# Wide attention spread over the narrow heads of the batch two before it, with norms batch by batch and their roots by Newton's method

## The chip, the cores and the metric

The kernel runs on one core of one Trainium2 chip. The metric is the device time in microseconds (us) from a launch; several runs are summed up by their median. The core has TensorE (PE in the profile, with its weight loads as PEld), VectorE (DVE), ScalarE (ACT), GpSimd (POOL) and SyncE (SP). Each engine works through its own queue in order; a semaphore makes one wait for another.

## The reference, cut to what matters

The input x has 8 batches of 512 tokens of width 128. All arithmetic is float32.

```
x = x + layernorm(attention(layernorm(x)))     # one wide head of 128, causal, rotary q and k
x = x + layernorm(ffn(layernorm(x)))
ffn(h): n = rmsnorm(h) * g1
        c = n @ w_down                         # 128 -> 64
        x' = h + attention of 16 narrow heads of width 4 over c, @ w_up
        t = rmsnorm(x') * g2
        probs = softmax(t @ router_w); top 2 of 8 experts, gates normalised
        return x' + sum over experts of gate * (silu(t @ w1) * (t @ w3)) @ w2
layernorm(x) = (x - mean) / sqrt(var + 1e-5);  rmsnorm(x) = x / sqrt(mean(x*x) + 1e-5)
```

## The kernel before, in words

Tokens lie on the 128 partitions, so a batch is NT = 4 tiles of 128x128. `x_all` and `h_all` hold all 32 tiles in on-chip memory. PSUM is dealt out as three buffers of two banks (tag `wide`), one single bank (tag `bank`), and one bank for the narrow heads' output (`po1`). All transposes and small products share the single bank; all score tiles share the three wide buffers.

**Stage 1, wide attention.** `ln_stats` takes mean and variance of 16 tiles at once (two groups of four batches), with a square root on ScalarE and a reciprocal on VectorE (`root`, L174). For each batch `attn_front` (L222) normalises, transposes, makes q and k (`pq`, each with a half-swapped copy, multiplied by the rotary table into `two` and added on POOL into `roped`) and v. `attn_back` (L248) makes causal scores two query tiles at a time, their negated maximum on VectorE, the exponential on ScalarE, transposes the probabilities (`pT`), multiplies by v (`po`) and by the output weights (`pr`). `between(gr)` (L302) then norms four batches, adds them to x and takes the norms of the next block. The loop at L732 issues the front of batch b+1 ahead of the back of batch b. This stage is ordered by the framework's own planner.

**Stage 2, narrow heads.** The order of this stage is written out by hand under `manual_schedule` (L837). A unit is one group of four heads of one batch: 8 batches x 4 groups = 32 units. `period(n)` (L758) interleaves three units: for v = n+1 the row-wise scores, which give each query's maximum (`rowwise`, `highest`: masks on TensorE, reduction on VectorE); for u = n the column-wise scores and exponentials (`columnwise`, `weights`: exponential on ScalarE) and their product with the values (`weigh`); for w = n+2 the copies into padded tiles on POOL (`values`, `queries`, `keys`) and the transposes through the single bank (`turn_q`, evacuated by VectorE; `turn_k` and `turn_m`, by ScalarE). `lower` splits the maxima into bf16 thirds on POOL, and `turn_m` of the next period reads them. A period uses the wide buffers eleven times, in the order 3A, 3C, 2A, (0,0), 2C, (0,1), 1AC, (1,0)+(3,0), 0AC, (1,1)+(3,1), 2; the letters are pairs of heads, the digits tiles of queries (row-wise) or of keys (column-wise).

Between these pieces stand calls of `aside()` (L747), four in a period. Each takes one step from a list of generators: `side` first, then `later`. On `side` come `ffn_front(b)` (L329: rms scaling `hs`, its transpose `hT`, the product `pc`, q, k and v `pqkv`, rotary, bf16 thirds on POOL) and `ffn_back(b)` (L552: `foT`, `pn`, `onT`, `pu`). On `later` comes `route(0)` (L588: rms statistics of 16 tiles with ScalarE's squares, router, top two).

**Stage 3, experts.** The planner orders `experts(b)` (L671), 64 experts-by-batch in all, with `route(1)` and, for each batch, `finish` (L719: layernorm, add on POOL, store).

Of the kernel before, what the change touches and what calls it, by code (L numbers as in the profile page):

```python
# [9 lines left out]
BF16 = mybir.dt.bfloat16  # L10
AF = mybir.ActivationFunctionType
# [3 lines left out]
P = 128  # L15
# [7 lines left out]
def kernel(  # L23
# [150 lines left out]
    def root(dst, src):  # L174

        sd = stat.tile([P, src.shape[1]], F32, tag="sd", name="sd")
        nc.scalar.activation(sd, src, AF.Sqrt)
        nc.vector.reciprocal(dst, sd)

    def ln_stats(src, n0, tag, n=GT):  # L180
# [5 lines left out]
        for i in range(n):  # L186
            nc.vector.bn_aggr(mv[:, i, :], st[:, i, :])
        ve = stat.tile([P, n], F32, tag="ve", name=f"ve_{tag}_{n0}")
        nc.vector.tensor_scalar(ve, mv[:, :, 1], EPS, None, ALU.add)
        rstd = stat.tile([P, n], F32, tag=f"rstd_{tag}", name=f"rstd_{tag}_{n0}")  # L190
        root(rstd, ve)
        return mv, rstd
# [7 lines left out]
    def rms_stats(src, n0, tag):  # L200

        ss = stat.tile([P, GT], F32, tag="ss", name=f"ss_{tag}_{n0}")
        for i in range(GT):
            sq = work.tile([P, D], F32, tag="sq", name=f"sq_{tag}_{n0}_{i}", bufs=1)
            nc.scalar.activation(
                sq, src[:, n0 + i, :], AF.Square, accum_out=ss[:, i : i + 1]
            )
        ve = stat.tile([P, GT], F32, tag="ve", name=f"vr_{tag}_{n0}")
        nc.vector.tensor_scalar(ve, ss, 1.0 / D, EPS, ALU.mult, ALU.add)
        rs = stat.tile([P, GT], F32, tag=f"rms_{tag}", name=f"rms_{tag}_{n0}")  # L210
        root(rs, ve)
        return rs
# [9 lines left out]
    def attn_front(b, st):  # L222
        xn = work.tile([P, NT, D], F32, tag="xn", name=f"xn_{b}")
        for t in range(NT):
            ln_apply(xn[:, t, :], x_all[:, b * NT + t, :], st, (b % GB) * NT + t)
        ps = transposed(xn, f"xnT_ps_{b}")
        xnT = work.tile([P, T], F32, tag="xnT", name=f"xnT_{b}")
        nc.scalar.copy(xnT, ps)
        roped = []
        for i in range(2):  # L230
# [3 lines left out]
            two = deep.tile([P, 2, T], F32, tag="pk", name=f"two_{b}_{i}", bufs=5)  # L234
            nc.vector.tensor_tensor(two, pq, ropea, ALU.mult)  # L235
            r = work.tile([P, T], F32, tag=f"roped{i}", name=f"roped_{b}_{i}")
            nc.gpsimd.tensor_tensor(r, two[:, 0, :], two[:, 1, :], ALU.add)  # L237
            roped.append(r)
        pv = bank(f"pv_{b}")
# [4 lines left out]
        v = work.tile([P, NT, D], F32, tag="v", name=f"v_{b}")  # L244
        nc.scalar.copy(v, pv.rearrange("p (t d) -> p t d", d=D))
        return roped[0], roped[1], v

    def attn_back(b, q, k, v):  # L248
        probs = []
        sums = work.tile([P, NT], F32, tag="sums", name=f"sums_{b}")  # L250
        for half in range(NT // 2):
# [8 lines left out]
            for i in range(2):  # L260
# [8 lines left out]
                probs.append(p)  # L269
        pT = work.tile([P, NT, T], F32, tag="pT", name=f"pT_{b}", bufs=1)  # L270
        for t in range(NT):
# [8 lines left out]
            )  # L280
        po = bank(f"po_{b}")
# [7 lines left out]
        nc.vector.reciprocal(rinv, sums)  # L289
        pr = bank(f"pr_{b}")  # L290
        for t in range(NT):
# [4 lines left out]
            h_all[:, b * NT : (b + 1) * NT, :],  # L296
# [3 lines left out]
        )  # L300

    def between(gr):  # L302

        n0 = gr * GT
        st = ln_stats(h_all, n0, "r")
        for i in range(GT):
            ln_apply(h_all[:, n0 + i, :], h_all[:, n0 + i, :], st, i)
        for b in range(GB):
            n = slice(n0 + b * NT, n0 + (b + 1) * NT)
            nc.gpsimd.tensor_tensor(x_all[:, n, :], x_all[:, n, :], h_all[:, n, :], ALU.add)  # L310
        st = ln_stats(x_all, n0, "h")
        for i in range(GT):
            ln_apply(h_all[:, n0 + i, :], x_all[:, n0 + i, :], st, i)
        return rms_stats(h_all, n0, "h")
# [14 lines left out]
    def ffn_front(b, rs):  # L329
        hs = work.tile([P, NT, D], F32, tag="xn", name=f"hs_{b}")  # L330
        for t in range(NT):
            i = (b % GB) * NT + t
            nc.vector.tensor_scalar(
                hs[:, t, :], h_all[:, b * NT + t, :], rs[:, i : i + 1], None, ALU.mult
            )
        yield
# [251 lines left out]
    def route(gr):  # L588
        n0 = gr * GT
        rs = rms_stats(h_all, n0, "t")  # L590
# [137 lines left out]
    sts = [ln_stats(x_all, 0, "x")]  # L728
    roots = []
    front = attn_front(0, sts[0])  # L730
# [27 lines left out]
    def period(n):  # L758
# [49 lines left out]
        if w:  # L808
            w.turn_q()
# [117 lines left out]
```

## Time and profile before

| what | us |
|---|---|
| median of 3 runs | 1009.24 (1004.33 to 1009.9) |
| the profiled execution | 1003.33 |
| its span, first to last instruction | 1001.5 |
| mean granted TensorE clock | 0.939 of full |
| first row-wise score of stage 2 starts | 219.05 |
| first expert product starts | 647.99 |
| TensorE / VectorE / ScalarE / POOL busy | 858.0 / 564.5 / 426.8 / 190.9 |

The page gives busy time of each engine and, in 40 slices of 25 us, busy tenths of each engine and the clock that TensorE was granted in tenths. A window row gives, for one stretch, its length, then for each engine the busy time with the number of instructions, then the granted clock, the DMA share and GB/s. A timeline row gives start, time, engine, line, operation, output <- inputs with shapes, and in brackets how long the engine was idle before it and what ended that.

### The profile page before, as it was taken

How to read it: one execution, taken by the hardware profiler on the slowest of the kernel's cores; microseconds unless marked ns; L12 is line 12 of the kernel's file. 1: busy time of each engine (PE TensorE's matmuls, PEld its weight loads, DVE VectorE, ACT ScalarE, POOL GpSimd, SP SyncE). 2: the span in 40 equal slices, each digit the busy share in tenths (PEclk: the TensorE clock that was granted, in tenths of full speed). 3: DMA queues.
4: the chain of work that ended last, by engine and by line, in shares of the span. 5: the costliest groups of instructions: out<-in, count | busy, mean ns of one | idle time of the engine just before them, and what ended most of it. 6: DMA issues, size and time to landing. Idle time of an engine off the chain costs nothing.

```text
span 1001.5 us, 14809 instructions
## 1 busy us (share of the span) xinstructions
PE 858.0 (86%) x5888; PEld 493.5 (49%) x5888; DVE 564.5 (56%) x1287; ACT 426.8 (43%) x668; POOL 190.9 (19%) x476
## 2 busy tenths in 40 slices
PE   2777568739989898986989988899999999999996
PEld 1444345414444444444444544366666666666664
DVE  6444773385666556564656675255654545545454
ACT  0212361234665566667665656542432323323231
POOL 5211211054242414141424221000000000000000
PEclk9999987657999999998999998899999999999999
DMA  9000000000000000000000000000000000000000
GB/s 252 1 0 1 0 1 0 1 1 1 1 2 2 1 1 2 2 2 1 1 1 2 1 1 1 1 2 0 11 11 1 11 1 11 11 1 11 1 11 10
DMA packets 14293, 9.34 MB, mean 9 GB/s; under 512 B 1200, under 2 KB 14064, under 8 KB 14224
## 3 DMA queue, kind: packets, MB, share of 16 engines
q1 hardware_dynamic: 12640, 7.34, 2.6%
q10 hardware_dynamic: 1296, 0.92, 0.3%
q8 instruction: 46, 0.75, 0.3%
q14 instruction: 23, 0.19, 0.1%
q0 software_dynamic: 288, 0.14, 0.1%
HBM read 6.30 MB, written 2.10 MB: 8 GB/s over the span
## 4 chain that ended last, share of the span: by engine, by line
PE 72%; ACT 10%; DVE 9%; issue 6%; DMA 2%; POOL 1%; SPq 0%; ACTq 0%; POOLq 0%; DVEq 0%
PE ph L677 20%; PE py L693 10%; PE po L544 8%; ACT pk L537 6%; PE sT L509 5%; PE sT L530 4%; PE sm L461 3%; PE po L283 3%; PE pq L233 3%; DVE nm L481 2%; PE sm L474 2%; DVE h_all L196 2%; PE mT_ps L432 2%; PE kT_ps L432 1%; PE pT_ps L274 1%
## 5 line engine op out<-in xcount | busy, mean ns | idle before, releaser
L481 DVE TENSOR_REDUCE nm<-sm 128x2 f32<-128x1024 f32 (+2 forms) x192 | 200.4, 1045 | 129.5 <-PE sm L474 125.5
L537 ACT ACTIVATE pk<-sT 128x1024 f32<-128x1024 f32 x160 | 163.6, 1027 | 89.9 <-PE sT L530 86.5
L685 ACT ACTIVATE sil<-ph 128x512 f32<-128x512 f32 x128 | 75.8, 597 | 228.1 <-PE ph L677 207.5
L686 DVE TENSOR_TENSOR hid<-sil,ph 128x512 f32<-128x512 f32 x128 | 87.5, 687 | 116.2 <-ACT sil L685 116.0
L693 PEld LDWEIGHTS py<-w2s,hid 128*128 128x128 f32 x1024 | 124.3, 192 | 31.6 <-issue 26.1
L677 PE MATMUL ph<-tT_all,w3s 128*128 128x512 f32 x256 | 131.3, 595 | 0.0
L677 PE MATMUL ph<-tT_all,w1s 128*128 128x512 f32 x256 | 131.1, 594 | 0.0
L693 PE MATMUL py<-w2s,hid 128*128 128x128 f32 x1024 | 124.8, 275 | 1.2 <-DVE h_all L702 1.2
L509 PE MATMUL sT<-mT,kT 39*128 39x384 bf16 (+3 forms) x512 | 67.1, 311 | 43.8 <-ACT pk L537 34.8
L544 PE MATMUL po<-pk,vpad 128*32 128x512 f32 (+3 forms) x1024 | 91.6, 454 | 0.0
L702 DVE SCALAR_TENSOR_TENSOR h_all<-py,gate_all,h_all 128x128 f32<-128x128 f32 x256 | 72.5, 344 | 28.4 <-PE py L693 28.2
L677 PEld LDWEIGHTS ph<-tT_all,w3s 128*128 128x128 f32 x256 | 48.2, 190 | 58.3 <-issue 58.2
L724 POOL TENSOR_TENSOR y<-y,x_all 128x512 f32<-128x512 f32 x8 | 10.2, 1271 | 349.0 <-DVE y L196 310.0
L461 PE MATMUL sm<-kT,qT 36*128 36x256 bf16 (+3 forms) x512 | 74.4, 312 | 2.3 <-ACT kT L439 1.4
L474 PE MATMUL sm<-mask_q,ident_bf 128*128 128x128 bf16 (+1 forms) x384 | 63.2, 248 | 0.0
L320 POOL CAST qpad<-nm 128x16 bf16<-128x16 f32 x32 | 8.1, 254 | 272.8 <-DVE nm L481 272.8
L530 PE MATMUL sT<-mask_k,ident_bf 128*128 128x256 bf16 (+1 forms) x320 | 58.5, 266 | 0.0
L509 PEld LDWEIGHTS <-kT 39*128 39x128 bf16 x512 | 27.7, 96 | 62.4 <-issue 57.9
L677 PEld LDWEIGHTS ph<-tT_all,w1s 128*128 128x128 f32 x256 | 43.5, 191 | 28.8 <-issue 18.8
L439 ACT COPY mT<-mT_ps 128x1024 bf16<-128x1024 bf16 x32 | 32.4, 1012 | 44.9 <-PE mT_ps L432 44.9
L461 PEld LDWEIGHTS <-qT 36*128 36x128 bf16 x512 | 21.3, 94 | 50.8 <-issue 40.1
L237 POOL TENSOR_TENSOR roped<-two 128x512 f32<-128x512 f32 x16 | 20.2, 1268 | 124.8 <-DVE two L235 124.8
(165 smaller groups left out, 1081.3 us busy)
## 6 DMA issues: line engine op xcount, KB each, us to landing
x_all<-in_L_attn_x_dram SPq DMA_DIRECT2D x8, 256.0 KB, 5.6
out_dram<-y SPq DMA_DIRECT2D x8, 256.0 KB, 2.3
w1s<-in_L_ffn_w_dram SPq DMA_DIRECT2D x2, 512.0 KB, 7.8
w3s<-in_L_ffn_w_dram SPq DMA_DIRECT2D x2, 512.0 KB, 7.4
w2s<-in_L_ffn_w_dram SPq DMA_DIRECT2D x2, 512.0 KB, 8.0
ropea<-in_rope_a_dram ACTq DMA_DIRECT2D x1, 512.0 KB, 5.2
wqk<-in_L_attn_wq_dram ACTq DMA_DIRECT2D x1, 64.0 KB, 3.3
wqk<-in_L_attn_wq_dram ACTq DMA_DIRECT2D x2, 32.0 KB, 4.4
```

Of the source, the lines that this page charges most:

```text
L461: nc.tensor.matmul(sc[:, i, c * n : (c + 1) * n], self.qT[at, pair, t * P : n], self.kT[at, pair, :n], start=(c == 0), stop=False,)
L474: nc.tensor.matmul(sc[:, i, : w * n].rearrange("p (c n) -> p c n", n=n)[:, :, t * P : n], ident_bf, mask_q.unsqueeze(1).to_broadcast([P, w ...
L481: nc.vector.tensor_reduce(self.nm[:, t, :].rearrange("p (c i) -> p i c", i=2)[:, :, pairs[0] : pairs[0] + w], sc[:, :, : w * n].rearrange( ...
L509: nc.tensor.matmul(sc[:, i, c : c + n], self.kT[at, pair, j * P : (j + 1) * P], self.mT[at, pair, j * P :], start=(c == 0), stop=False,)
L530: nc.tensor.matmul(blocks[:, i, :: max(last // P, 1), :], ident_bf, mask_k.unsqueeze(1).to_broadcast([P, len(parts), P]), start=False, sto ...
L537: nc.scalar.activation(p[:, :, :c], sc[:, :, :c], AF.Exp, scale=HD**-0.5)
L544: nc.tensor.matmul(po[h * HP : (h + 1) * HP, j * P :], vpads[self.g][:, j, h, :], self.p[j, h // 2][:, h % 2, :], start=(self.g == 0 and j ...
L677: nc.tensor.matmul(ph[:, i, :], w[:, e, c * P : (c + 1) * P], tT_all[:, b, :], start=True, stop=True,)
L685: nc.scalar.activation(sil, ph[:, 0, :], AF.Silu)
L686: nc.vector.tensor_tensor(hid[:, c, :], sil, ph[:, 1, :], ALU.mult)
L693: nc.tensor.matmul(py[:, t * P : (t + 1) * P], hid[:, c, t * P : (t + 1) * P], w2s[:, e, c, :], start=(c == 0), stop=(c == FC - 1),)
L702: nc.vector.scalar_tensor_tensor(h_all[:, n, :], py[:, t * P : (t + 1) * P], gate_all[:, n, e : e + 1], h_all[:, n, :], ALU.mult, ALU.add,)
```

## The change

Stage 1 is gone as a stage. `attn_front`, `attn_back`, `between` and the scaling of `ffn_front` become one generator, `attend(b)`, whose last part is the rest of `ffn_front`. It has 24 places at which it hands back, so it is done in 24 steps and a remainder. Ahead of the units, batch 0 does eight steps alone and is then alternated with batch 1 until batch 0's narrow inputs are made; the rest of batch 1 goes on `side`. At the first unit of batch b, `attend(b + 2)` goes on `side`. A period calls `aside()` seven times in place of four.

The norms are taken for four tiles of one batch rather than 16. A root is an integer first guess and three Newton steps on VectorE, 14 operations, with no ScalarE square root anywhere in the kernel. The rms norm that follows the second layernorm is taken from the same variance: `hs` is made from x in one ScalarE operation, so its 16 squares and the later scaling are gone. `finish` and `route` use the new root too.

`two`, `roped` and `v` have one buffer each; `two` no longer shares the buffers of `pk`.

```diff
-    def root(dst, src):
-        sd = stat.tile([P, src.shape[1]], F32, tag="sd", name="sd")
-        nc.scalar.activation(sd, src, AF.Sqrt)
-        nc.vector.reciprocal(dst, sd)
+    def root(x, tag):
+        ts, tt = nc.vector.tensor_scalar, nc.vector.tensor_tensor
+        n = x.shape[1]
+        y = stat.tile([P, n], F32, tag=f"root_{tag}", name=f"root_{tag}")
+        a = stat.tile([P, n], F32, tag="newton", name=f"newton_{tag}")
+        ts(a.bitcast(I32), x.bitcast(I32), 1, None, ALU.logical_shift_right)
+        ts(y.bitcast(I32), a.bitcast(I32), -1.0, float(0x5F3759DF), ALU.mult, ALU.add)
+        for _ in range(3):
+            tt(a, y, y, ALU.mult)
+            tt(a, a, x, ALU.mult)
+            ts(a, a, -0.5, 1.5, ALU.mult, ALU.add)
+            tt(y, y, a, ALU.mult)
+        return y
...
-    def attn_front(b, st):
+    def attend(b):
+        n0 = b * NT
+        tiles = slice(n0, n0 + NT)
+        st = ln_stats(x_all, n0, "x")
         xn = work.tile([P, NT, D], F32, tag="xn", name=f"xn_{b}")
         for t in range(NT):
-            ln_apply(xn[:, t, :], x_all[:, b * NT + t, :], st, (b % GB) * NT + t)
+            ln_apply(xn[:, t, :], x_all[:, n0 + t, :], st, t)
+        yield
         ps = transposed(xn, f"xnT_ps_{b}")
         xnT = work.tile([P, T], F32, tag="xnT", name=f"xnT_{b}")
         nc.scalar.copy(xnT, ps)
+        yield
...
-            two = deep.tile([P, 2, T], F32, tag="pk", name=f"two_{b}_{i}", bufs=5)
+            two = work.tile([P, 2, T], F32, tag="two", name=f"two_{b}_{i}", bufs=1)
...
+            yield      # after each of pq 0 and 1, after v, after each half of the scores,
+                       # after each of four pT, after oT
...
         nc.vector.tensor_tensor(h_all[:, tiles, :], ...)
+        yield
+
         st = ln_stats(h_all, n0, "r")
+        yield
+        for i in range(NT):
             ln_apply(h_all[:, n0 + i, :], h_all[:, n0 + i, :], st, i)
+        nc.gpsimd.tensor_tensor(x_all[:, tiles, :], x_all[:, tiles, :], h_all[:, tiles, :], ALU.add)
+        yield
+        yield
+        mv = moments(x_all, n0, "h")
+        ve = stat.tile([P, 2 * NT], F32, tag="ve2", name=f"ve2_{b}")
+        nc.vector.tensor_scalar(ve[:, :NT], mv[:, :, 1], EPS, None, ALU.add)
+        nc.vector.tensor_scalar(ve[:, NT:], mv[:, :, 1], 1.0 + EPS, EPS**2, ALU.mult, ALU.add)
+        both = root(ve, "h")
+        shift = stat.tile([P, NT], F32, tag="shift", name=f"shift_{b}")
+        nc.vector.scalar_tensor_tensor(shift, mv[:, :, 0], -1.0, both[:, NT:], ALU.mult, ALU.mult)
+        yield
+        hs = work.tile([P, NT, D], F32, tag="xn", name=f"hs_{b}")
+        for t in range(NT):
+            ln_apply(h_all[:, n0 + t, :], x_all[:, n0 + t, :], (mv, both), t)
+            nc.scalar.activation(
+                hs[:, t, :], x_all[:, n0 + t, :], AF.Identity,
+                bias=shift[:, t : t + 1], scale=both[:, NT + t : NT + t + 1],
+            )
+        yield
+        yield from ffn_front(b, hs)
...
-        if u and u.g == 2 and u.b + 2 < B:
-            side.append(ffn_front(u.b + 2, roots[(u.b + 2) // GB]))
+        if u and u.g == 0 and u.b + 2 < B:
+            side.append(attend(u.b + 2))
...
+        aside()      # added in three places: ahead of turn_m, behind turn_q, behind turn_k
...
     with tc.manual_schedule():
-        side.append(ffn_front(1, roots[0]))
+        first, second = attend(0), attend(1)
+        for _ in range(8):
+            next(first)
+        while 0 not in made:
+            next(first, None)
+            next(second, None)
+        side.append(second)
```

## The prediction

> **What bounds the kernel.** I read the page's busy rows and slices first, then its windows per stage, then single periods of the narrow heads, then timelines.
>
> ```profile
> PE 858.0 (86%) x5888; PEld 493.5 (49%) x5888; DVE 564.5 (56%) x1287; ACT 426.8 (43%) x668; POOL 190.9 (19%) x476
> ...
> PE   2777568739989898986989988899999999999996
> DVE  6444773385666556564656675255654545545454
> PEclk9999987657999999998999998899999999999999
> ```
>
> Three stages: up to about slice 9 (0 to 219 us) the wide attention, TensorE seven tenths busy at a clock that sinks to half; 219 to 648 us the 32 units of narrow heads, TensorE at nine tenths; then the experts, where TensorE never rests and nothing the change does to ScalarE or VectorE shows. So two terms decide: what the first stage gives back, and what the second pays to take its work in.
>
> I marked the units by the first POOL cast of `lower` (L320) and asked for busy time between the marks:
>
> ```profile
> core 0: us, PE busy (x) PEld busy (x) DVE busy (x) ACT busy (x) POOL busy (x), PEclk, DMA share, GB/s
> ...
> 397.08:410.46 13.38, 11.57 (x123) 6.12 (x124) 7.57 (x8) 7.47 (x9) 2.88 (x12) 1.00 0.01 2
> 410.46:422.41 11.95, 11.56 (x117) 5.54 (x117) 7.57 (x11) 8.20 (x10) 2.88 (x11) 1.00 0.01 2
> 422.41:435.58 13.17, 11.36 (x119) 6.07 (x120) 8.14 (x10) 7.31 (x9) 7.84 (x16) 1.00 0.01 1
> 435.58:447.36 11.78, 10.51 (x115) 5.26 (x116) 7.70 (x9) 7.53 (x9) 3.43 (x13) 1.00 0.01 2
> 447.36:468.19 20.83, 13.49 (x127) 7.49 (x128) 8.62 (x14) 17.11 (x46) 2.87 (x12) 0.84 0.00 1
> ...
> 608.95:623.47 14.52, 12.80 (x120) 6.65 (x120) 7.57 (x8) 8.82 (x17) 2.88 (x11) 0.85 0.00 1
> 623.47:637.80 14.33, 12.45 (x101) 4.53 (x100) 6.28 (x6) 7.14 (x7) 1.00 (x4) 0.74 0.00 1
> ```
>
> A period's floor is 11.78 us with 10.5 of TensorE and 7.7 of VectorE. The first four rows are a clean batch: 50.3 us. Side work of TensorE is hidden or not by its place: hT and pc (1.9 us, between the 2A to 1AC scores) cost 0.2 us, while onT and pu (1.55 us, around the period's seam) cost 1.6. The row of 20.83 is the best evidence on a burst: route's 16 squares and two table loads, 10.9 us of ScalarE in one slot, cost 20.83 - 13.38 = 7.5 us (that period has onT and pu as well), and the clock fell to 0.84. Bursts of 1.5 us on VectorE (route's small operations) cost nothing.
>
> **The first stage.** Before, the first narrow scores start at 219.0 us. After, only batch 0 runs alone, then batch 1 alternates with it. From the rows, for batch 0: x lands 4.4 us; statistics, root and normalising on VectorE to 9.7; transposes and copy to 11.7; pq, two, roped to 21.3 (the second pq waits for `two`, now one buffer); scores, exponentials and their table load to 28. Then VectorE's order puts batch 1's first step (5.3 us) ahead of pT of batch 0, and so on: po at 42, r statistics 46 to 50, x add 54, moments to 59, hs 61, hT 63, pc 66, pqkv 72, rope and splits on POOL to 79; moments of batch 1 (to 85) stand ahead of qT's copy; kT follows: scores at about 87. Gain 132 us, give or take 10. Loads are issued as before; no DMA moves.
>
> **A batch with attention in it.** Counted from rows: TensorE gets pq 8x0.43, scores 3.0, pT 1.55, po 2.1, pv and pr 0.9 each, xnT 0.6: 12.5 us. VectorE gets two 2x1.22, nmax 1.95, pT 1.95, the h product 0.69, and three norms. The root has 14 dependent operations. No row shows it; the nearest are the tail's small ones:
>
> ```profile
> 995.02 0.17 DVE L189 TENSOR_SCALAR ve_o<-mv_o 128x4 f32<-128x4 f32 x1
> 995.22 0.20 ACT L177 ACTIVATE sd<-ve_o 128x4 f32<-128x4 f32 x1 [5.58 <-DVE ve_o L189]
> 995.46 0.18 DVE L178 RECIPROCAL rstd_o<-sd 128x4 f32<-128x4 f32 x1 [0.27 <-ACT sd L177]
> 995.73 1.12 DVE L196 TENSOR_SCALAR y<-h_all,mv_o,rstd_o 128x128 f32<-128x128 f32 x4
> ```
>
> A small operation lasts 0.17 and its dependent starts 0.03 later: 14x0.20 = 2.8 us. (Ends: 1.0 at the 0.07 pitch of independent bn_aggr, 3.5 at the 0.25 of 16-wide ones; dependence takes 2.8.) So three bursts: x 0.87+0.36+0.2+2.8+1.1 = 5.3; r 4.2, then 1.3 for applying it; h 4.7, then 1.1. With hs gone to ScalarE (-0.87), VectorE rises by about 23 us, from 31 to 54 a batch; TensorE from 45 to 57.5. Neither is over 72, so the floor doesn't decide; the queues do.
>
> There are 7 slots a period, 28 a batch; attention with ffn_front takes 24, ffn_back 4, so every step has a fixed place. Walking the queues with three wide PSUM buffers and one bank:
> - First period of a batch (x statistics, ffn_back, xnT, pq0): the 5.3 us burst sits ahead of the reduction of 3C. Two later score tiles wait behind it, the third finds no buffer, turn_q waits for pn's bank: 3.9 us. Behind turn_k, pu needs the bank that the kT copy still reads:
>
> ```profile
> 359.21 0.61 PE L432 MATMUL kT_ps<-ident_bf,kpad 128*128 128x128 bf16 x8
> ...
> 359.76 0.39 PE L509 MATMUL sT<-mT,kT 39*128 39x256 bf16 x4
> ...
> 360.18 1.01 ACT L439 COPY kT<-kT_ps 128x1024 bf16<-128x1024 bf16 x1
> ...
> 361.40 0.39 PE L461 MATMUL sm<-kT,qT 36*128 36x512 bf16 x2
> ```
>
>   Before, sT at 359.76 used the time to 361.19; now pu stands there: 1.4 wait + 0.93 + 1.0 for pu's bank + 0.6 xnT + 1.7 pq0 = 5.7.
> - Second: pq1 1.7; pv 0.9; both score halves with nmax and exponentials taking turns on VectorE and ScalarE while each holds a wide buffer, 3.4; pT1 behind turn_k 1.7; pT2 0.5. Sum 8.2.
> - Third and fourth: pT3 directly ahead of turn_m 1.6; po 2.3; pr 0.9; r burst, its apply, h burst, then hs and hT that wait for it: VectorE's order holds 15 us of work between qT and the next 3C where 8.6 stood, 8.0 with hT. Moments also wait on VectorE for POOL's x add; the reduction of 3A queues behind them, and TensorE's (0,0) scores want its buffer. pc 0.2; pqkv 1.5. Sum 14.5.
>
> Total 4x11.78 + 9.6 + 8.2 + 14.5 = 79.4 us; I take 79. From below: exposure as with the old side work, about half of TensorE's, and bursts half absorbed, 66. From above: 88 with clock losses.
>
> **Clock.** The burst row fell to 0.84, and the last two periods before the experts ran at 0.85 and 0.74 and took 14.5 and 14.3 instead of 11.8. The Trainium skill ("TensorE: Matmul & The Clock Gate", Part 1) says the array drops to half rate after an idle window of about 3.4 us and needs a busy one to come back; this speaks against the change, whose bursts idle TensorE 3 to 4 us. By the rule each of three stalls a batch may cost half a window, 1.7 us: up to 5 a batch, 30 in all. The burst row shows a lower clock only with a stall of 7.5 us. I take the row, so nothing in the sum, and keep 30 for the high side; the rule would make the sum up to 1073.
>
> **Other edits.** Roped and x adds (3x1.27 us a batch) join POOL's queue ahead of `lower` and `queries`; POOL is busy 3 to 8 of 12 us, cover enough; uncovered they delay turn_m by 1.3. hs on ScalarE (4x0.31) fits its 4.3 us idle; if not, 1.2 a batch. Route(0) gets slots only once attention is done: its cost, about 8 us, moves into units 24 to 27, no longer inside the 315.5 us counted below but after it. Its two table loads go: 2.6 us by the row of 1283 ns; "ScalarE: Activation LUTs" (What ACT_TABLE_LOAD costs) adds a drain, 2.66 us each, 5.3. In the trace the next instruction starts 0.02 us after a load, so I take 2.6, already off those 8; by the rule the sum would be 2.7 lower. In the experts the loads go for free and seven roots hide behind TensorE (VectorE has 2.7 us free of each 5.2 us expert; +1 us, up to 20 if not). The last root is bare: 2.8 in place of 0.54, +2.3.
>
> **Sum.** Units 0 to 23 took 546.90 - 231.38 = 315.5 us. 6x79 - 315.5 = +158.5; -132; +8; +2.3; +1: +38 us. The profiled execution took 1003.33 (span 1001.5): 1041. The runs shown lie 0.1 to 0.7% above that execution; I predict 1043. Break-even is a batch of (315.5 + 132 - 11.3)/6 = 72.7 us.
>
> **Rivals.** (1) Faster: the steps fall into waits that TensorE has anyway. For it: hT and pc cost 0.2 for 1.9 us; TensorE needs only 57.5. At 66 us a batch it gives -40, 963; it wins from below 72.7. Against: pu, xnT, pq0, pq1, pv, po stand at the seam, where no idle time is. (2) Lower clock: 88 a batch, +92, 1095. For it: 0.84 in the burst row; against: TensorE is still 70% busy. (3) The start doesn't shrink as counted: the DVE chain of two batches runs to 110 us: +22, 1063. (4) The two terms cancel, 1003 to 1009.
>
> **Chances.** Mine 0.48 (own range 1015 to 1075), (1) 0.28, (2) 0.10, (3) 0.09, (4) 0.05: my walk adds waits one by one, and some may fall together, so (1) gets most of the rest. Within 0.5% is about what cannot be told from no change: faster 0.28, same 0.05, slower 0.67. The range 975 to 1088 leaves out the better half of (1) and most of (2).
>
> **What would show it.** First scores at 87 us; a batch of four periods at 79 us, with idle TensorE before turn_m, behind turn_k, and behind reductions that wait for norms; VectorE 54 us a batch; the expert stage at 345 us. Wrong if a batch comes under 73 us, or the clock row sinks throughout.

## The result, and the profile after

| | before | after | change | predicted |
|---|---|---|---|---|
| median of the runs, us | 1007.2 (1004.33 to 1009.9) | 1122.1 (1120.38 to 1129.74) | ratio 1.116 (1.109 to 1.122) | 1043 |
| span of the profiled execution | 1001.5 | 1121.1 | +119.6 | +38 |
| mark of the first unit (first POOL cast of `lower`) | 231.38 | 109.66 | -121.7 | -132 |
| units 0 to 23 | 315.5 | 529.9 | +214.4 | +158.5 |
| units 24 to 30 | 90.9 | 115.35 | +24.4 | +8 |
| from the mark of the last unit to the end | 363.7 | 366.2 | +2.5 | +3.3 |

The median before is of four executions, one more than in the table ahead of the prediction. The second execution of experiment 5 below ran at a lower granted clock than its first (0.899 against 0.922) and 1.9% longer, so that experiment has one time.

The change is slower, as forecast, by three times the forecast 38 us; 1122 lies outside the range of 975 to 1088. The expert stage came out as counted, and the start gained 10 us less. Most of the loss is in the units: the six batches with attention beside them took 88.3 us each (529.9 / 6) in place of 79, the first of them 79.1 and the other five 89.0 to 90.6, and the units behind them 16 us more than counted.

The page of the changed kernel: the busy row, the slices of the clock, and the engines of the chain that ended last.

```profile
PE 908.7 (81%) x5888; PEld 510.6 (46%) x5888; DVE 644.2 (57%) x1745; ACT 390.3 (35%) x590; POOL 191.6 (17%) x476
...
PEclk9766898787688888788878786989999999999998
...
PE 65%; DVE 21%; ACT 7%; issue 6%; POOL 1%; DMA 0%; POOLq 0%; ACTq 0%; DVEq 0%
```

TensorE has the same 5888 matmuls as before and is busy 51 us longer: the same work at a lower clock. The row of the clock holds 6 to 8 through the whole stage of the heads, where it held 9. VectorE's share of the chain rose to 21%, from the 9% that the page of the kernel before gives.

The windows between the marks, same columns as before (length, then busy time and instructions of PE, PEld, DVE, ACT and POOL, then the granted clock): one batch of four periods, and the two long periods behind the last batch.

```profile
458.66:477.86 19.20, 13.17 (x114) 6.72 (x114) 13.83 (x36) 8.16 (x11) 7.17 (x16) 0.73 0.01 1
477.86:505.17 27.31, 23.13 (x155) 12.29 (x155) 11.81 (x15) 10.48 (x18) 5.45 (x14) 0.86 0.00 1
505.17:529.65 24.48, 20.27 (x170) 9.76 (x169) 13.71 (x39) 9.65 (x11) 4.09 (x12) 0.88 0.00 1
529.65:548.92 19.27, 12.66 (x95) 6.50 (x96) 13.50 (x39) 8.08 (x12) 4.16 (x14) 0.73 0.00 1
639.56:659.86 20.30, 13.32 (x114) 6.93 (x114) 10.21 (x24) 15.67 (x51) 7.17 (x17) 0.75 0.00 1
678.45:699.88 21.43, 18.94 (x137) 10.07 (x136) 9.26 (x19) 8.72 (x10) 2.89 (x12) 0.66 0.01 2
```

The four sum to 90.3 us. VectorE is busy 52.9 of them (predicted 54). TensorE is busy 69.2, where the work counted at the fast rows' durations was 57.5: some 12 us of busy time are the clock. The trace confirms it. The granted clock is 0.50 in four stretches of this batch (466.54 to 476.78, 480.20 to 487.02, 504.09 to 510.92 and 531.40 to 541.64 us) and full in the rest. TensorE is busy for 24.4 us in the four; at full clock half of that, 12.2 us, would go, and 57.0 would be left. It stands idle for 21 us, which is about what the walk through the queues had (79.4 - 57.5 = 22). So the idle time was predicted, as a total, and the busy time was not.

The marks put what stands behind the turn of the keys into the next window. In those terms the prediction had 11.78 + 3.9 = 15.7 us for the first period, 11.78 + 5.7 + 6.0 = 23.5 for the second (8.2 less the 2.2 of pT1 and pT2, which fall into the third), and 40.3 for the third and fourth together. Measured: 19.2, 27.3 and 43.8. Each is 3.5 to 3.8 us over.

The timeline around the two predicted stalls, TensorE and VectorE (start, duration, line, instruction; in brackets the idle time before it and what ended it). First the x norms' burst, then the place behind the turn of the keys in another batch.

```profile
462.92 0.90 DVE L204 TENSOR_SCALAR ve_x<-mv_x 128x4 f32<-128x4 f32 x1
463.27 0.38 PE L538 MATMUL sT<-mT,kT 39*128 39x512 bf16 x2
...
466.92 0.16 DVE L185 TENSOR_TENSOR newton_x<-newton_x,ve_x 128x4 f32<-128x4 f32 x1
467.12 0.17 DVE L186 TENSOR_SCALAR newton_x<-newton_x 128x4 f32<-128x4 f32 x1
...
469.82 0.61 PE L538 MATMUL sT<-mT,kT 39*128 39x512 bf16 x2 [4.44 <-DVE nm L510]
...
387.64 1.75 PE L608 MATMUL pu<-wup,onT 64*128 64x128 f32 x8 [1.41 <-ACT kT L468]
390.17 1.12 PE L229 MATMUL xnT_ps<-ident,xn 128*128 128x128 f32 x4 [0.78 <-DVE h_all L612]
391.22 0.61 PE L538 MATMUL sT<-mT,kT 39*128 39x256 bf16 x4
391.76 0.61 PE L559 MATMUL sT<-mask_k,ident_bf 128*128 128x256 bf16 x2
392.30 1.94 PE L573 MATMUL po<-pk,vpad 128*32 128x512 f32 x8
```

The waits are the predicted ones: sT behind the reduction that queues behind the burst, pu behind the copy of kT (1.4 predicted, 1.41 measured), xnT behind pu's bank. The prices after them are not. The same pair of sT lasts 0.38 us ahead of the stall and 0.61 us behind it; behind pu, everything runs at that rate. This is how the clock is read most sharply: one instruction of one shape, before and after a wait.

### The profile page after: what moved, and what is told of

Same layout as the page of the kernel before. It is cut to its first block, busy times and chain, and to the rows that moved or that the text cites. A ratio compares the mean times of both kernels' runs of the same rounds, so it can differ in the third digit from the quotient of the medians.

```text
span 1121.1 us, 15129 instructions
## 1 busy us (share of the span) xinstructions
PE 908.7 (81%) x5888; PEld 510.6 (46%) x5888; DVE 644.2 (57%) x1745; ACT 390.3 (35%) x590; POOL 191.6 (17%) x476
## 4 chain that ended last, share of the span: by engine, by line
PE 65%; DVE 21%; ACT 7%; issue 6%; POOL 1%; DMA 0%; POOLq 0%; ACTq 0%; DVEq 0%
PE ph L706 18%; PE py L722 9%; PE po L573 6%; DVE nm L510 4%; PE sT L538 3%; PE sT L559 3%; PE sm L490 3%; PE pq L249 3%; ACT pk L566 2%; PE sm L503 2%; PE po L301 2%; PE sc L272 2%; ACT kT L468 1%; PE pc L371 1%; DVE nmax L280 1%
## 5 line engine op out<-in xcount | busy, mean ns | idle before, releaser
L510 DVE TENSOR_REDUCE nm<-sm 128x2 f32<-128x1024 f32 (+2 forms) x192 | 199.5, 1043 | 121.0 <-PE sm L503 120.3
L722 PEld LDWEIGHTS py<-w2s,hid 128*128 128x128 f32 x1024 | 124.3, 192 | 31.6 <-issue 25.4
L538 PE MATMUL sT<-mT,kT 39*128 39x128 bf16 (+3 forms) x512 | 75.5, 344 | 46.1 <-DVE nm L510 24.6
L573 PE MATMUL po<-pk,vpad 128*32 128x512 f32 (+3 forms) x1024 | 104.6, 508 | 0.0
L490 PE MATMUL sm<-kT,qT 36*128 36x256 bf16 (+3 forms) x512 | 77.5, 330 | 22.0 <-ACT p L282 8.5
L706 PEld LDWEIGHTS ph<-tT_all,w3s 128*128 128x128 f32 x256 | 47.9, 190 | 57.4 <-issue 57.3
L503 PE MATMUL sm<-mask_q,ident_bf 128*128 128x128 bf16 (+1 forms) x384 | 68.3, 265 | 0.0
L559 PE MATMUL sT<-mask_k,ident_bf 128*128 128x256 bf16 (+1 forms) x320 | 64.4, 289 | 0.0
L490 PEld LDWEIGHTS <-qT 36*128 36x128 bf16 x512 | 23.9, 95 | 80.5 <-issue 69.7
L461 PEld LDWEIGHTS <-qpad 128*128 128x128 bf16 x512 | 36.2, 108 | 44.4 <-issue 17.8
L251 DVE TENSOR_TENSOR two<-pq,ropea 128x1024 f32<-128x1024 f32 x16 | 19.6, 1225 | 53.7 <-PE pq L249 52.3
```

Of the source, the lines that this page charges most:

```text
L490: nc.tensor.matmul(sc[:, i, c * n : (c + 1) * n], self.qT[at, pair, t * P : n], self.kT[at, pair, :n], start=(c == 0), stop=False,)
L503: nc.tensor.matmul(sc[:, i, : w * n].rearrange("p (c n) -> p c n", n=n)[:, :, t * P : n], ident_bf, mask_q.unsqueeze(1).to_broadcast([P, w ...
L510: nc.vector.tensor_reduce(self.nm[:, t, :].rearrange("p (c i) -> p i c", i=2)[:, :, pairs[0] : pairs[0] + w], sc[:, :, : w * n].rearrange( ...
L538: nc.tensor.matmul(sc[:, i, c : c + n], self.kT[at, pair, j * P : (j + 1) * P], self.mT[at, pair, j * P :], start=(c == 0), stop=False,)
L559: nc.tensor.matmul(blocks[:, i, :: max(last // P, 1), :], ident_bf, mask_k.unsqueeze(1).to_broadcast([P, len(parts), P]), start=False, sto ...
L573: nc.tensor.matmul(po[h * HP : (h + 1) * HP, j * P :], vpads[self.g][:, j, h, :], self.p[j, h // 2][:, h % 2, :], start=(self.g == 0 and j ...
```

## The experiments

After the result two theories stood. The clock theory: each wait of TensorE is followed by a stretch at half clock, and that work is on the path, so a burst costs more than its wait. The queue theory, mine so far: the low clock only shows that TensorE idles, and the loss is waits alone, more of them or longer than I had walked through. An interval (the ratio to the kernel before, 95%) is given where a verdict hangs on it; elsewhere the differences that a reading rests on are many times the scatter of the runs.

### 1. The burst alone

To the kernel before: the x norms' statistics, Newton root and four scalings on VectorE, once a batch, ahead of the turn of the lowered queries. Work added, nothing removed; the result is unread.

```diff
+        if u and u.g == 0:
+            burst(u.b)      # 4 bn_stats, 4 bn_aggr, 15 small operations, 4 scalings
         if u:
             u.turn_m()
```

> The kernel before, with only a VectorE burst added: at the first unit of each batch, ahead of turn_m, it takes the statistics of four tiles, a Newton root of 14 operations and four normalisings into a scratch tile that nobody reads. Eight bursts of the kind that the wide attention's first step makes. Clock theory (each burst idles TensorE 4 to 4.5 us and costs some 3 us more by a lower clock behind it): +7 us a burst, about +56 us, and granted clock in those periods near 0.75. Queue theory (the burst idles TensorE and nothing else): +4 us a burst, about +32 us, clock unchanged near 0.98. If bursts don't matter: under +10 us.

Measured: 1069.7 us, +63 on 1006.7 (ratio 1.061, 1.054 to 1.069); 63 / 8 = 7.9 us for a burst of 6.0 (6.8 to 8.6 by the interval). In the two profiled executions the units alone, from the first mark to the last, took 478.0 us where they took 406.4, 8.9 a burst; the first unit began 5.8 us earlier than before, which the bursts do not explain. A period with it and the next one (windows), and TensorE behind it (timeline):

```profile
344.71:362.58 17.87, 13.00 (x112) 6.45 (x112) 12.50 (x36) 7.63 (x9) 3.45 (x13) 0.77 0.00 0
362.58:377.16 14.58, 12.76 (x128) 6.38 (x128) 7.57 (x8) 7.61 (x8) 2.89 (x11) 0.94 0.00 1
```

```profile
354.63 0.61 PE L511 MATMUL sT<-mT,kT 39*128 39x512 bf16 x2 [3.21 <-DVE nm L483]
...
365.57 0.39 PE L463 MATMUL sm<-kT,qT 36*128 36x512 bf16 x2
```

17.87 us where the clean period has 11.78, 14.58 where it has 13.38. A wait of 3.2 us, and then half clock for 10.2 us (354.19 to 364.43 by the granted clock). The cost is near the clock theory's figure and twice the queue theory's. A period with 4 us of VectorE to spare (7.70 busy of 11.78 in the clean row) doesn't absorb the burst: it costs its length and 2 to 3 us more.

### 2. The root as one operation

From the changed kernel. This leaves the root out (a straight line in the variance stands in its place), so the time is that of the norms without 13 of their 14 operations for a root.

```diff
-        ts(a.bitcast(I32), x.bitcast(I32), 1, None, ALU.logical_shift_right)
...
+        nc.vector.tensor_scalar(y, x, -0.5, 1.5, ALU.mult, ALU.add)
```

> The changed kernel with the 14-operation root replaced by one VectorE operation (a straight line in place of the inverse square root, so this leaves the root itself out). Bursts of VectorE shrink by 3 to 3.5 us each. If the bursts and the clock behind them carry the loss: three bursts a batch, each about 3 us of idle and 2 to 3 us of clock cheaper, about -16 us a batch, 1122 to about 1010 to 1030. If TensorE's work and bank waits at the period's seam carry it: -5 us a batch or less, about 1085 to 1095.

Measured: 1051.8, 70 us less than the changed kernel; a batch 81.9 (15.4, 27.8, 22.8, 16.0). Three roots of 13 operations at 0.20 us are 7.8 us; the batch lost 8.4. VectorE's roots stand on the path one for one. Neither forecast came true: 8.4 us a batch is half of the 16 and more than the 5. What went is idle time of TensorE, from 21.0 to 13.9 us a batch; its busy time only fell from 69.2 to 68.0. So shorter bursts took their waits away and left the low clock nearly as it was.

### 3. The slot behind the turn of the keys

From the changed kernel: the slot in which TensorE waited for kT's copy and for pu's bank is called behind the first weighing.

```diff
             w.turn_k()
-        aside()
...
             u.weigh(0)
         aside()
+        aside()
```

> The changed kernel with the step behind turn_k moved behind weigh(0), so that pu and pT of tile 1 no longer wait for the kT copy ahead of the last column-wise scores. My step of the prediction said 1.4 us of wait at each of two such places a batch, and 1.0 for pu's own bank: -17 to -23 us in all by the queue alone, -35 us if the clock behind these waits goes up too, and about 0 if the wait is only moved to another place (the next score tile waits for kT in any case).

Measured: 1090.6, 31.6 us less; a batch 85.4 (19.4, 24.7, 21.5, 19.8). The second and third periods, which begin with what stood in that slot, lose 2.6 and 3.0 us, where the waits at their heads were 1.4 + 0.8 and 1.1. The sum is nearer to the figure with the clock than to that of the queue alone.

### 4. Newton's method in the kernel before

```diff
-        nc.scalar.activation(sd, src, AF.Sqrt)
-        nc.vector.reciprocal(dst, sd)
+        # shift, subtract from the constant, three rounds of four operations
```

> The kernel before with only the root changed to Newton's method on VectorE: stage order, group size and everything else as before. Ahead: five roots 16 wide cost about 3.3 us each on VectorE, in place of a square root with table loads of 1.28 us; in the heads route's burst loses 2.6 us of table loads; the last root costs +2.3 us. Sum between -5 and +8 us; a loss over 15 us would say that the roots by themselves hurt in the experts, where seven of them stand ahead of work for TensorE.

Measured: 1012.2 (1.0075, 1.0049 to 1.0100), +5.5. Where norms are taken 16 tiles at a time in a stage of their own, the method costs little. With experiment 2 this says that its place in the head units makes it dear.

### 5. Half the burst

As experiment 1 without the 14 operations of the root (the scaling uses the variance itself); 2.9 us on VectorE.

> The kernel before with the same added burst as in the first experiment but without its 14 root operations (the normalising uses the variance itself; nobody reads the result): about 2.9 us of VectorE in place of 6.0. Clock theory with a threshold: a burst that TensorE can ride out with its spare score buffers leaves it waiting under 1.5 us and the clock full, +1 to +2 us a burst, +8 to +16 us in all, far less than half of the +63 of the long burst. If cost is proportional to the burst: +30 us.

Measured: 1028.2, +25 on the profiled execution of before: 3.1 us for 2.9. From the first mark to the last it is 436.8 us for 406.4, 3.8 a burst (here, too, the first unit began 5.8 us earlier). That is nearer to the proportional figure than to the threshold's: a burst of 2.9 us is not free. TensorE in a period with it, and three windows around the slow stretch:

```profile
344.91 0.39 PE L510 MATMUL sT<-mT,kT 39*128 39x512 bf16 x2 [0.42 <-DVE nm L482]
346.80 0.61 PE L433 MATMUL qT_ps<-ident_bf,qpad 128*128 128x128 bf16 x8 [1.16 <-DVE o_nat L566]
347.65 0.64 PE L510 MATMUL sT<-mT,kT 39*128 39x384 bf16 x4
...
355.39 0.39 PE L462 MATMUL sm<-kT,qT 36*128 36x512 bf16 x2
```

```profile
344.05:347.46 3.41, 1.73 (x20) 0.99 (x21) 3.38 (x6) 1.08 (x2) 0.00 (x0) 1.00 0.00 0
347.46:354.29 6.83, 6.41 (x42) 2.91 (x42) 2.59 (x4) 3.74 (x4) 1.69 (x8) 0.50 0.00 0
354.29:357.70 3.41, 3.41 (x42) 1.53 (x34) 1.23 (x1) 1.03 (x3) 1.18 (x5) 1.00 0.03 7
```

Waits of 0.4 and 1.2 us, and then half clock for 6.8 us: an sT group of 384 columns takes 0.64 where the same takes 0.40 at full clock (the changed kernel at 521.6 us). The Trainium skill ("TensorE: Matmul & The Clock Gate", Part 1) puts the fall behind an idle window of about 3.4 us. In experiment 1 the trace agrees: in the 3.42 us ahead of the fall TensorE is busy for 0.34. Here it is busy for 1.73 of 3.41 us, and the clock falls all the same, so a window that is half idle was enough. The slow stretches of both experiments are a whole number of such windows, three (10.2 us) and two (6.8 us).

### 6. The root by ScalarE and VectorE

From the changed kernel: `activation(sd, x, AF.Sqrt)` and `reciprocal(y, sd)` in place of the 14 operations, the norms where they are.

> The changed kernel with its root undone: square root on ScalarE and reciprocal on VectorE, four or eight wide, in place of Newton. VectorE loses 12 operations a root (-2.5 to -3.5 us a burst); ScalarE gains two table loads a root, 2.6 us, ahead of exponentials. If VectorE's bursts are the cause and ScalarE's are no worse: 1122 to 1070 to 1090. If the table loads stall as much as the operations did: within 10 us of 1122. In the run with one operation for the root the kernel came to 1052, which bounds the gain.

Measured: 1074.1 (-48). A batch takes 81 to 85 (the last: 17.8, 26.7, 22.9, 17.9). Two thirds of what experiment 2 gained are had with a real root, table loads and all.

### 7. All bursts cut up

From the changed kernel, many edits at once: Newton rounds of three operations, x norms a batch ahead in pieces beside the rotary and the splits, r and h norms over two steps each, pT 0 and 1 in one step, the slot moved as in 3, the router's squares two at a time.

```diff
         nc.gpsimd.tensor_tensor(rot, straight, crossed, ALU.add)
+        ahead = 0 < b < B - 1
+        if ahead:
+            mv, ve = variance(x_all, (b + 1) * NT, "x")
         yield
+        if ahead:
+            y, a = guess(ve, "x", 1)
```

> The changed kernel with the same computation, its bursts cut up and its steps moved: statistics and root of x for the next batch in the slots where ffn_front only uses POOL; r and h norms one piece per slot with three operations per Newton round in place of four; step behind turn_k moved behind weigh(0); pT of tiles 0 and 1 in one slot, ffn_back's blank gone, so nothing that uses the single bank stands right ahead of turn_m; hs behind mT's copy; route's 16 squares two at a time. If bursts with the clock they cost (some 70 us by the one-operation root) and the bank waits (32 us by the moved slot) carry the loss, a batch falls from 90 to 66 to 74 us and the time to 975 to 1025. If attention's own TensorE work and its PSUM turns carry it, it stays above 1050.

Measured: 1094.2 (1.0878, 1.0839 to 1.0917): a miss. Batches take 84.2 and 86.5 by turns, no less than with the moved slot alone. Two things show in the trace. The first is in the timeline of VectorE and POOL:

```profile
451.66 1.27 POOL L424 TENSOR_TENSOR straight<-straight,crossed 128x512 f32<-128x512 f32 x1
451.80 1.16 DVE L187 TENSOR_SCALAR newton_x<-ve_x 128x4 int32<-128x4 int32 x1
452.99 0.17 DVE L188 TENSOR_SCALAR root_x<-newton_x 128x4 int32<-128x4 int32 x1
...
453.71 1.27 POOL L378 TENSOR_TENSOR left<-straight,thirds 128x512 f32<-128x512 f32 x1
453.88 1.12 DVE L180 SCALAR_TENSOR_TENSOR root_x<-newton_x,root_x 128x4 f32<-128x4 f32 x1
...
456.66 1.27 POOL L381 TENSOR_TENSOR thirds<-left,thirds 128x512 bf16<-128x512 f32 x1
456.82 1.12 DVE L180 SCALAR_TENSOR_TENSOR root_x<-newton_x,root_x 128x4 f32<-128x4 f32 x1
```

Three operations of four elements a partition last 1.1 us instead of 0.17, and each ends within 0.03 us of a POOL operation that began just before it. The Trainium skill ("SBUF — State Buffer", Terms) says that VectorE and GpSimd share a pair of ports which one of them holds for its whole instruction; this trace agrees, at 1.0 us an encounter. I had moved the norms to where POOL is busiest.

Three encounters are 3 us a batch, far from the 10 us or more that are missing. The second is the clock, here over one whole batch:

```profile
450.50:536.95 86.45, 71.15 (x534) 37.16 (x531) 52.60 (x121) 36.55 (x49) 20.90 (x54) 0.81 0.00 1
```

TensorE now stands idle for 15.3 us a batch, where it was 21.0 in the changed kernel and 19.2 in experiment 3. But it is busy for 71.2, more than in either (69.2 and 66.2), and the clock is as low as in the changed kernel. Cutting the bursts up made the waits shorter and did not bring the clock back. Which of the many edits did that, no run says.

### 8. A filled wait

Back to the clock. From the changed kernel: 18 matmuls whose output nobody reads stand where TensorE waited for the x norms' burst.

```diff
             v.rowwise(2, C)
+        if u and u.g == 0 and u.b + 2 < B:
+            keep_busy(u, 18)      # 128x512 bf16 into the accumulator's bank
```

> The changed kernel, with 18 matmuls of nothing (128x512 bf16 each, into the accumulator bank that is free there, their output unread) ahead of the columns' scores of the second half in the first period of each batch with attention, where TensorE stood for 4.4 us behind the x norms' burst: work added, none taken away. At 0.21 us each they are 3.9 us inside the wait. Clock theory: TensorE does not fall to half clock there, the 10 us that follow run at 0.39 rather than 0.61 us an sT pair, 3 to 4 us a batch, 1095 to 1105 in all. If the slow matmuls come from what runs beside them (the evictions of VectorE and ScalarE, the PSUM buffers) or from the wait's length only, nothing falls: 1122 to 1135.

Measured: 1121.8, no change (1122.1). The clock did what the theory says and the time did not:

```profile
465.77 3.83 PE L773 MATMUL spare<-qT 128*128 128x512 bf16 x17 [0.16 <-issue]
470.03 0.39 PE L538 MATMUL sT<-mT,kT 39*128 39x512 bf16 x2 [0.43 <-DVE nm L510]
...
479.29 1.12 PE L229 MATMUL xnT_ps<-ident,xn 128*128 128x128 f32 x4 [0.78 <-DVE h_all L612]
480.34 0.61 PE L538 MATMUL sT<-mT,kT 39*128 39x256 bf16 x4
```

sT is back at 0.39. The window 458.89 to 476.29 is 17.4 us at clock 1.00, where 19.2 at 0.73 stood: 1.8 us of 3 to 4 hoped for; TensorE then waits for VectorE's o_nat and reductions. Behind the next two waits, kT's copy and pu's bank, the clock is down again and the second period is 27.4, as it was. In the first and the last units longer periods took back the rest; what lengthened them I have not found.

### 9. Square root and moved slot together

Experiments 3 and 6 in one kernel.

> The changed kernel with two of the parts put right that were tried singly: the roots of the norms by ScalarE's square root and VectorE's reciprocal (alone: 1074, so -48) and the slot behind the turn of the keys moved behind the first weighing (alone: 1091, so -32). If the two take away different waits, the gains add: 1035 to 1050. If both take away the same low-clock stretches, the second gives less than half of its own: 1058 to 1072.

Measured: 1041.7 (1.034, 1.026 to 1.041), 80 us less than the changed kernel; the parts alone gave 31.6 and 48. They add, so they remove different waits. A batch is 78.5 (15.6, 25.4, 20.7, 16.8), still above the break-even of 72.7, and the kernel is still slower than before.

### 10. Filling the waits of the first stage

The kernel before, with such matmuls ahead of pT, po, pr and the first turn of the heads in its last four batches.

```diff
+            if b >= GB and t:
+                keep_busy(f"pT_{b}_{t}", 3)
             ps = bank(f"pT_ps_{b}_{t}")
...
+        keep_busy("heads", 40)
```

> The kernel before, with matmuls of nothing in the waits of its first stage: for the last four batches of the wide attention 3 ahead of each transpose of the weights from the second on, 3 ahead of the weighted sum, 4 ahead of the output projection, and 40 ahead of the first turn of the narrow heads, where TensorE stood for 12.5 us. Clock theory: the granted clock of 110 to 245 us (0.50 to 0.93) comes to near 1; where TensorE is in the chain (150 to 190 us, then from the first turn on) that is 6 + 3 us, half of some 10 in 190 to 231, and 4 in the first head units: 985 to 998. If the low clock there is only a consequence of the waits and costs nothing, the added work shows: 1005 to 1020.

Measured: 1004.9 (0.9961, 0.9928 to 0.9994). It missed its aim, and tells nothing of the clock. The tile's view of the 40 that should fill the wait for qpad, and the wait itself:

```profile
L219 PE MATMUL spare_heads<-ident_bf x40: 377/379/379, 75.8 to 97.7; 128*128 128x512 bf16 x40
```

```profile
PE qT_ps L447 <- POOL qpad L421: 13.5, 1, 13.5
```

They depend on nothing, and the planner of this stage put them at 76 to 98 us, more than 100 us ahead of their wait, which is as long as ever; the others came early too (19 to 75 us). Why this kernel is 0.4% quicker is open. In the profile its first unit begins at 225.4 us in place of 231.4, but so it does in experiments 1 and 5, which leave this stage as it was.

### 11. The router's squares in steps

As 10, and the 16 squares of the router's root in pairs, a slot each.

```diff
                 sq, src[:, n0 + i, :], AF.Square, accum_out=ss[:, i : i + 1]
             )
+            if i % 2:
+                yield
```

> As the one before, and the router's root of the first four batches taken in steps: its 16 squares two at a time on ScalarE, each pair in a slot of its own between the narrow heads, where they stood as one burst and that period took 20.8 us against 13. 6 to 8 us less than the run before it if the burst was what made that period long; the same within 2 us if the router's other steps did.

Measured: 1001.4 (0.9916, 0.9879 to 0.9953): the quickest kernel here, though by less than 1% of the time before, and by 3.5 us rather than 6 to 8 on experiment 10. Windows of the period where the burst was, and of two later ones, from an execution that took 1005.8:

```profile
443.43:457.46 14.03, 12.89 (x123) 6.91 (x124) 7.57 (x8) 9.61 (x22) 2.87 (x11) 0.88 0.01 1
551.56:568.29 16.73, 15.59 (x132) 8.70 (x132) 8.54 (x13) 9.42 (x18) 2.88 (x12) 0.78 0.00 1
568.29:585.32 17.03, 16.24 (x131) 8.50 (x130) 7.85 (x12) 8.61 (x10) 2.87 (x12) 0.71 0.01 1
```

20.83 us became 14.03: the squares were the burst. But the router's steps come later, and two periods that took 13.67 and 13.43 now take 16.7 and 17.0 at a clock of 0.78 and 0.71. In these windows the gain of one place was lost in another.

### 12. Three filled waits

Experiment 8 in five batches, and 7 + 4 more such matmuls in the waits behind the turn of the keys.

```diff
             w.turn_k()
+        if u and u.g == 0 and 0 < u.b < B - 2:
+            busy[0] = w.qT
+            keep_busy(f"k_{u.name}", 7)
         aside()
...
+        if b >= 3:
+            keep_busy(f"xnT_{b}", 4)
         ps = transposed(xn, f"xnT_ps_{b}")
```

> The changed kernel with matmuls of nothing in three waits of the first period of five batches: 18 where the x norms' burst stands (as in the run with one filling), 7 behind the turn of the keys ahead of pu, 4 between pu and xnT; that is 2.3 us more in waits of 1.4 and 0.8 us. In the changed kernel what follows these two waits runs back to back at half clock (sT 0.61, mask 0.61, weighing 1.94, pq 3.08, in place of 0.39, 0.39, 1.06 and some 1.8). If the low clock is on the path there, the second period falls from 27.3 to about 24.5 us, with the first 4 to 5 us a batch, 1097 to 1104 in all. If another wait takes up the gain, as the run with one filling showed in part, the second period stays above 26.5 and the whole at 1112 to 1124.

Measured: 1103.6 (1102.3 to 1104.2), 18.5 us less than the changed kernel with 29 matmuls a batch more. Windows of the first two periods of a batch, and the timeline behind the turn of the keys:

```profile
447.44:465.43 17.99, 16.18 (x133) 7.63 (x135) 12.99 (x36) 7.98 (x10) 7.14 (x16) 0.91 0.01 1
465.43:490.34 24.91, 22.52 (x165) 12.22 (x163) 11.81 (x15) 10.56 (x18) 5.44 (x14) 0.96 0.00 1
```

```profile
466.53 1.16 PE L618 MATMUL pu<-wup,onT 64*128 64x128 f32 x8
467.61 1.04 PE L237 MATMUL spare_xnT<-qT 128*128 128x512 bf16 x4
468.49 0.64 PE L229 MATMUL xnT_ps<-ident,xn 128*128 128x128 f32 x4
469.06 0.39 PE L548 MATMUL sT<-mT,kT 39*128 39x256 bf16 x4
469.38 0.39 PE L569 MATMUL sT<-mask_k,ident_bf 128*128 128x256 bf16 x2
469.70 1.06 PE L583 MATMUL po<-pk,vpad 128*32 128x512 f32 x8
```

The waits for kT and the bank are as long as before; only nothing is idle in them. What follows takes 0.64, 0.39, 0.39 and 1.06 us where it took 1.12, 0.61, 0.61 and 1.94. The two periods sum to 42.9 us where they summed to 46.5, and the batch of four is 86.0 where it was 90.3. Here TensorE's work stands back to back, so its clock is on the path. This is the direct proof: work added, time gone.

### 13. The turn ahead of hs

From the changed kernel. The waits name mT's copy for the longest wait of the fourth period (hT, 3.6 to 4.0 us), and in ScalarE's queue that copy stands behind the four hs. In that period alone the turn now comes ahead of the slot.

```diff
+        ahead = u and u.g == NG - 1
+        if not ahead:
+            aside()
         if u:
             u.turn_m()
+        if ahead:
+            aside()
```

> The changed kernel with one edit: in the fourth period of a batch the turn of the lowered queries stands ahead of the slot with hs and not behind it, so ScalarE copies mT before the four hs and not after them. The chain of waits names mT's copy for hT's wait of 3.6 to 4.0 us. If the place in ScalarE's queue is the cause, 3 us a batch go: 1100 to 1106. If VectorE's h norms, which hs and the first reduction both wait for, are behind it, hT waits nearly as long for hs: under 1 us a batch, 1114 to 1122.

Measured: 1124.3, no gain. The wait of hT in the changed kernel, and now:

```profile
PE hT_ps L229 <- ACT mT L468: 3.6, 1, 3.6
PE hT_ps L229 <- ACT hs L342: 1.7, 1, 1.7
```

The wait is shorter and has another name; the batch from 283.97 to 373.33 is 89.4, 0.9 us less than the one shown. hs itself waits for the h norms on VectorE, and so does the first reduction. The name in the waits was the last in a chain, not its cause.

## Why the prediction was wrong, point by point

**The clock: the step that failed.** "I take the row, so nothing in the sum." The row was the one burst of before, with a stall of 7.5 us, and I concluded that stalls of 3 to 4 would not do it. So a term of 12.2 us a batch stood in the sum as nothing. Experiments 1 and 5 show the fall after waits of 3.2 and of 1.2 us, for 10.2 and 6.8 us; beyond its own length the burst costs 2 to 3 us in experiment 1, and in experiment 8 its stretch is worth 1.8; and experiment 12 got 3.6 us a batch back in two of the four periods by filling the waits alone. The rule of the skill that I weighed and set aside gave "up to 5 a batch": the right way, and less than half of the 12.2. I had counted three stalls at half a window each; the batch shown has four slow stretches of two or three windows. The trace of before had the answer, too. In the row at 0.85 that I printed, the clock is half from 619.20 us on, and no wait in the 3.4 us ahead of that is longer than 1.14 us. And in the first stage, the same eight matmuls, lines I had not laid side by side:

```profile
176.25 2.42 PE L283 MATMUL po<-pT,v 128*128 128x512 f32 x8 [0.56 <-DVE pT L277]
...
186.71 4.64 PE L283 MATMUL po<-pT,v 128*128 128x512 f32 x8 [0.78 <-DVE pT L277]
```

Between the two there is no wait above 0.82 us, only many; the second takes nearly twice as long.

**The rival that came true.** Rival 2 had 88 us a batch and 1095. The batches took 88.3. The other 27 us are the start (10) and the units behind the batches (16). I gave it 0.10, on the argument that TensorE is still 70% busy. In the batch shown it is 77% busy, at a clock of 0.81.

**What absorbs a burst.** The walk charged 3.9 us for a burst of 5.3. Alone, 2.9 us cost 3.1 to 3.8 and 6.0 cost 7.9 to 8.9; in the changed kernel, 7.8 us of root operations came out as 8.4. A period has four free microseconds of VectorE, but the burst stands ahead of reductions that hold TensorE's buffers, so it can't use them.

**The x burst's size.** Predicted 5.3, measured 6.9 (461.75 to 468.63): 14 operations at 0.20 hold where POOL is quiet (0.17 at 467.12, the next 0.20 later), but next to POOL's splits single ones took 0.24 to 0.90. +1.6 us.

**The account of a batch.** 10.8 us over in the batch shown: 7.3 in the first two periods, of which 3.6 is the clock by experiment 12 and 1.6 the longer burst; 2.1 is not divided further. 3.5 is in the third and fourth. Half clock shows there as well (po at 508.03 takes 1.94 us), and experiment 13 rules out ScalarE's order, but no run divides those 3.5.

The granted clock divides whole batches in another way. Each row is one batch with attention; "work" is TensorE's busy time with the half-clock stretches counted at half, "low clock" is what they add, and the rest is idle.

| us | batch | work | low clock | idle |
|---|---|---|---|---|
| predicted | 79.4 | 57.5 | 0 | 22 |
| the changed kernel | 90.3 | 57.0 | 12.2 | 21.0 |
| 2, root as one operation | 81.9 | 57.0 | 11.0 | 13.9 |
| 3, moved slot | 85.3 | 57.3 | 8.9 | 19.2 |
| 7, bursts cut up | 86.5 | 56.8 | 14.4 | 15.3 |
| 9, square root and moved slot | 78.5 | 57.7 | 8.3 | 12.5 |
| 12, three filled waits | 86.0 | 57.2 and 6.3 of no use | 7.9 | 14.6 |

By this account the clock is the whole miss of a batch, since the idle time is 1 us under the walk's. It is an account and no experiment: at full clock some waits would grow, as in experiment 8. In experiment 12 they did not: the matmuls of no use and the idle time together are 20.9 us, as the idle time was, and the batch is shorter by 4.3 us, which is what "low clock" fell by (12.2 to 7.9). For those 7.9 us no run shows how much a higher clock would give back.

**The units behind the batches.** +8 predicted, +24.4 measured. I counted the router's burst by its row of before. (That row's slot is 9.7 us of ScalarE, 452.25 to 461.98, not the 10.9 that I read.) In the changed kernel the squares come in a period that also has 10.2 us of VectorE, where the row had 8.6, and the windows above have 20.3 and 21.4 us at clocks of 0.75 and 0.66. No run takes these apart; experiment 11 only shows that the router's other steps can sit in periods 3 us longer than before.

**The start.** First scores at 98 us, not 87: -121.7 for -132. No run takes the start apart.

**Right.** The sign; VectorE at 54 us a batch (52.9); idle TensorE of 22 us (21), though only as a total; the waits behind the turn of the keys (1.4 and 0.8, and 1.1 for pT1); Newton's pitch of 0.20, with some luck (the 0.03 us between two operations was read from VectorE to ScalarE; the one pair within VectorE in those lines, 995.46 and 995.73, has 0.09); the experts and the end (+2.5 for +3.3); the break-even batch of 72.7, which even the repaired version (78.5) doesn't reach.

## What to carry to other kernels

When a change puts waits into a stream of matmuls that was dense, so that TensorE idles for half of some 3.4 us, price the work behind them at the slow clock for 7 to 10 us, and read that clock from one instruction of one shape in the trace, not from a mean over a long window. A busy engine with idle time left doesn't absorb a burst if the burst stands ahead of what frees another engine's buffers. Where tiny VectorE operations are to be spread out, keep them away from POOL's long ones.

## What I had not expected of the hardware

- Waits of 0.4 and 1.2 us within 2.4 us were followed by half clock for 6.8 us (experiment 5), one of 3.2 by 10.2 us (experiment 1).
- The clock changed on a grid: in all fifteen traces every slow stretch between two changes lasts a whole number of times 3.41 us.
- Matmuls with no use, in a wait, made the kernel 18.5 us quicker (experiment 12); the same idea with one wait of three filled gave nothing (experiment 8).
- A VectorE operation on four elements a partition took 1.1 us instead of 0.17 beside a POOL operation of 1.27 us, three times in 6 us (experiment 7).
